# A graph-transformer kernel: tail work placed by a table of openings instead of an even pace

## The chip, the cores and the metric

The program runs on one core of one Trainium2 chip. The metric is device time in microseconds (us) of one execution. The engines are TensorE (PE: matmuls; its weight loads are PEld), VectorE (DVE), ScalarE (ACT), GpSimd (POOL) and SyncE (SP, which here only issues DMAs). [...]

## The reference, cut to what matters

Input x has 16 graphs of 1024 nodes and 128 features, adj is a sparse 1024 x 1024 adjacency matrix (about 8 neighbours a node). Four layers follow one another. Layers 0, 2 and 3 are attention over the neighbours with 8 heads of 16, each with a feed-forward part; layer 1 is graph attention (GAT) with one head. An attention layer is

```python
Q, K, V = h @ Wq, h @ Wk, h @ Wv                 # 8 heads of 16
attn = softmax(where(adj == 0, -inf, Q K^T / 4)) # over neighbours alone
x = layer_norm(h + attn @ V @ Wo + bo)
x = layer_norm(x + relu(x @ W1 + b1) @ W2 + b2)  # W1 is 128x256
...
h = x @ W; e = leaky_relu(h @ a_src + (h @ a_dst).T)
x = layer_norm(softmax(where(adj == 0, -inf, e)) @ h + x)   # layer 1
```

## The kernel before

**Units.** A layer is cut into two groups of 8 graphs (g = 0, 1) and 8 tiles of 128 nodes (t = 0 to 7), so there are 4 x 2 x 8 = 64 units (l, g, t); 48 are attention and 16 are GAT. Keys and values of all nodes of a group stand in a table in HBM. For each tile, rows of neighbours are gathered from that table by POOL's indirect DMA, one neighbour of each of 128 nodes a gather (1 MB in an attention layer).

**Parts.** A unit's gathers are worked off in parts: pairs of gathers, and one single gather that stands fourth (the "mixed" part, index 3). An attention unit has five parts, but six at t = 0 and four at t = 7. The main loop runs over all parts i of all units. In an attention unit one turn issues, in this order:

- `products(i)` (L958, DVE): gathered keys times queries, into one of four `pr` buffers;
- `summed(i-2)` (L1025, PE): weighted values added up over neighbours; frees `pr` buffers. Parts 0 and 1 of a unit are summed together, in the turn of part 3;
- after a unit's last part, `divided` first issues PE's sums of the exponentials (L1025, `ps<-ex,marks`);
- first call of `others()`;
- `exponentials(i)` (L981 reduce on DVE, L985 exp on ACT), then, in a unit's part 1, the next unit's `queries` and the load after it are put on their lists;
- second call of `others()`;
- `weighted(i-1)` (L1009, DVE), then `gathered(i+3)` (L946, POOL: issues the gathers three parts ahead into the ring of four `e` buffers);
- in a unit's part 1: the previous unit is closed (`divided` goes on with a reciprocal, L1062, and two multiplications, L1065, on DVE, which make `o` for the two halves of the graphs and create two tails);
- third call of `others()`.

I call a call of `others()` an **opening**: it is where all work that isn't the gather-multiply-sum stream is slipped in. A five-part unit has 15 of them.

**Tails.** A tail is a Python generator, `attention_tail(l, g, t, h, o)`, one for each half h of the 8 graphs (a: h = 0, b: h = 1). Each `yield` ends a step. In the kernel before a tail has 13 steps: transpose o (PE) with its copy (ACT) and the bias on x (ACT); Wo (8 matmuls); squares for the norm (ACT); `rstd` and scaling (ACT); transpose to x1; W1 with ReLU, both halves of the hidden layer; W2 (12 matmuls); squares; rstd and scaling; transpose to the new x; keys and values of two graphs; of two more; the table's DMA. Half b yields once at the start, and so runs one step behind a. In the last layer the end is a transpose back and an indirect DMA to `out` by POOL (L691), once for both halves. Before a unit is closed, all earlier tails must have handed back a flag "free" (given at the transpose to the new x; in the last layer it is never given, and the tails are run to their end).

**The pace.** At each closing, `pace` is set so that 13 less `LATE` (1 in layer 0, 2 in layers 2 and 3) steps are spread evenly over the openings of the unit. When it is due, `advance(tails)` moves every tail on by one step.

**The front.** Each opening also does one step of the first generator that has work among `fronts` (the next unit's `queries`, 4 steps: Wq for one half and the copy of q; 4 matmuls L909 that spread q over partitions and 4 copies L912; the same for the other half), `loads`, and, while layer 0 works on group 0, `at_leisure`: the transposes and projections of group 1 of the input.

**Buffers.** Four PSUM banks `ps` are shared by everything short-lived. `yps` has two banks, `acc` one tile, `pr` four, `e` four, and `f1` (the hidden layer) one.

Of the kernel before, what the change touches and what calls it, by code (L numbers as in the profile page):

```python
# [137 lines left out]
def sparse_path(ctx: ExitStack, tc: tile.TileContext, a: dict, out: bass.AP, flag):  # L138
# [20 lines left out]
    for j in range(J):  # L159
        q = slice(32 * j, 32 * j + 32)  # L160
# [452 lines left out]
    def normed(y, dve=False):  # L613

        z = twos.tile([P, GH, D], F32, tag="o", name="z")
        total = smalls.tile([P, GH], F32, tag="total", name="total")
        if dve:
            nc.vector.tensor_copy(z, y)
            nc.vector.tensor_tensor(z, z, y, ALU.mult)
            nc.vector.tensor_reduce(total, z, mybir.AxisListType.X, ALU.add)  # L620
            nc.vector.tensor_scalar(total, total, 1.0 / D, EPS, ALU.mult, ALU.add)
        else:
            for i in range(GH):
                nc.scalar.activation(  # L624
                    z[:, i, :], y[:, i, :], AF.Square, scale=D**-0.5, bias=root,
                    accum_out=total[:, i : i + 1],
                )
        yield
        rstd = smalls.tile([P, GH], F32, tag="rstd", name="rstd")
        nc.scalar.activation(rstd, total, AF.Ln)  # L630
        nc.scalar.activation(rstd, rstd, AF.Exp, scale=-0.5)
        if dve:
            nc.vector.tensor_tensor(
                z, y,
                rstd.rearrange("p (g o) -> p g o", o=1).to_broadcast([P, GH, D]), ALU.mult,
            )
            return z
        for i in range(GH):
            nc.scalar.activation(z[:, i, :], y[:, i, :], AF.Copy, scale=rstd[:, i : i + 1])  # L639
        return z  # L640
# [62 lines left out]
    def attention_tail(l, g, t, h, o):  # L703
        layer = LAYERS[l][0]
        p = {n: w[layer, n] for n in ATTN if (layer, n) in w}
        xt = xs[l, g, t][:, h]
        last = (l, g, t) == units[-1]
        dve = last and h > 0
        for _ in range(0 if last else h):
            yield  # L710
        oT = twos.tile([P, GH, P], F32, tag="oT", name="oT")
        turned(o, oT, dve=dve)

        if dve:
            nc.vector.tensor_scalar(xt, xt, p["bo"], None, ALU.add)
        else:
            nc.scalar.activation(xt, xt, AF.Identity, bias=p["bo"])
        yield
        ps = ybanks.tile([P, GH, D], F32, tag="yps", name="yps")
        for i in range(GH):  # L720
            nc.tensor.matmul(ps[:, i, :], oT[:, i, :], p["Wo"], start=True, stop=False)  # L721
            nc.tensor.matmul(ps[:, i, :], xt[:, i, :], centre, start=False, stop=True)  # L722
        yield
        z = yield from normed(ps, dve)
        yield
        x1 = twos.tile([P, GH, P], F32, tag="oT", name="x1")
        turned(z, x1, p["ln1_g"], p["ln1_b"], dve)
        yield
        f1 = (queries_of_shared if dve else hidden)().rearrange("p (f c) -> p f c", f=F)
        for f in range(F):  # L730
            ps = bank([P, GH * P])
            nc.tensor.matmul(  # L732
                ps, p["W1"][:, f * P : (f + 1) * P], x1.rearrange("p g n -> p (g n)"),
                start=True, stop=True,
            )
            if dve:
                nc.vector.tensor_scalar(
                    f1[:, f, :], ps, p["b1"][:, f : f + 1], 0.0, ALU.add, ALU.max
                )
            else:  # L740
                nc.scalar.activation(f1[:, f, :], ps, AF.Relu, bias=p["b1"][:, f : f + 1])  # L741
        yield
        ps = ybanks.tile([P, GH, D], F32, tag="yps", name="yps")
        for i in range(GH):
            for f in range(F):
                nc.tensor.matmul(  # L746
                    ps[:, i, :], f1[:, f, i * P : (i + 1) * P], p["W2"][:, f, :],
                    start=(f == 0), stop=False,
                )
            nc.tensor.matmul(ps[:, i, :], x1[:, i, :], centre, start=False, stop=True)  # L750
        yield
# [58 lines left out]
    def at_once(g):  # L810
# [12 lines left out]
        for t in range(T):  # L823
# [9 lines left out]
            while both:  # L833
                advance(both)
                yield

    def exponents():
        return exps.tile([P, MOST * G * H], F32, tag="ex", name="ex")

# [40 lines left out]
    def queries(u):  # L880
# [15 lines left out]
        for h in range(HF):  # L896
            q = ones_.tile([P, GH * D], F32, tag="q", name="q")
            ps = bank([P, GH, D])
            for i in range(GH):
                nc.tensor.matmul(  # L900
                    ps[:, i, :], xs[l, g, t][:, h, i, :], w[LAYERS[l][0], "Wq"],
                    start=True, stop=True,
                )
            nc.scalar.copy(q, ps.rearrange("p g d -> p (g d)"))  # L904
            yield
            pss = []
            for j in range(J):
                ps = bank([P, GH * D])
                nc.tensor.matmul(ps, rep_of(j), q[32 * j : 32 * j + 32], start=True, stop=True)  # L909
                pss.append(ps)  # L910
            for j in range(J):
                nc.scalar.copy(qs[u][:, j, h * GH * D : (h + 1) * GH * D], pss[j])  # L912
            yield

    def shared(u):

# [136 lines left out]
    def divided(u):  # L1053
# [9 lines left out]
        for h in range(HF):  # L1063
# [7 lines left out]
                ALU.mult,  # L1071
            )
            tails.append((attention_tail if heads > 1 else graph_tail)(l, g, t, h, o))
        nc.scalar.copy(both[:, 0, :], den)
        yield
        n = G * heads
# [2 lines left out]
    tails = []  # L1079
# [12 lines left out]
                free.append(gen)  # L1092

    pace = [0.0, 0.0]

    def idle():
        return slow if held[0] or not busy[0] else []

    def others():
        pace[0] += pace[1]  # L1100
        while pace[0] >= 1.0:
            advance(tails)
            pace[0] -= 1.0
        while True:
# [10 lines left out]
        for _ in range(eager[0]):  # L1115
            advance(idle())

    eager = [1]

    with tc.manual_schedule():  # L1120
# [39 lines left out]
        for i in range(len(parts) + 2):  # L1160
# [45 lines left out]
                    pass  # L1206
            if closing is not None and here:
                while any(gen not in free for gen in tails):
                    advance(tails)
                next(closing)  # L1210
                sizes, closing = closing, None
                passes = 3 if is_attention(u) else 4
                steps = STEPS if is_attention(done) else GRAPH_STEPS
                steps -= LATE[units[done][0]]
                pace[:] = 0.0, steps / (passes * sum(part[0] == u for part in parts) - 1)
            others()
            if i + 1 >= len(parts) or parts[i + 1][0] != u:

                while fronts:
                    advance(fronts)  # L1220
        while tails:
            advance(tails)
        for _ in closing:
# [438 lines left out]
```

## Time and profile before

| | us |
|---|---|
| median of 3 runs | 2250.97 (2247.27 to 2253.18) |
| the profiled execution | 2254.23 |
| its span in the profile | 2251.9 |
| busy: PE / DVE / ACT / POOL | 2043.1 / 1872.9 / 1528.3 / 1016.3 |
| PE weight loads | 1271.3 |
| mean granted clock of PE | 0.962 of full speed |

The span starts with the first instruction of the profile and ends with the last; 2.3 us of the execution's time lie outside it. Busy shares are averages over layers with different limits. [...] Layers show in the trace by the reciprocal (L1062) that closes each unit: layer 0's group 1 lies around 484 to 704 us, GAT from about 731 to 1042 us, layer 2 to about 1633 us, layer 3 to 2215 us, and then the last unit's tail to the end.

### The profile page before, as it was taken

To read this page: it belongs to the slowest core of one execution; us is meant where nothing else is said; L and a number is where in the kernel's file an instruction comes from. 1 tells how busy PE (TensorE), PEld (TensorE's weight loads), DVE (VectorE), ACT (ScalarE), POOL (GpSimd) and SP (SyncE) were. 2 spreads that over 40 slices of the span, in tenths; PEclk is the share of its full clock that TensorE was granted. 3 is DMA by queue.
4 is the path that set the end of the run, shared out by engine and by line. 5 is a ranking of instruction groups with operands and counts; after the bars stand their busy time and mean duration, and the time that the engine had idled before them with its cause. 6 is when DMAs were issued, how large, how long until landed. Compare 5 with 4: busy or idle time off the path is not lost.

```text
span 2251.9 us, 36507 instructions
## 1 busy us (share of the span) xinstructions
PE 2043.1 (91%) x13140; PEld 1271.3 (56%) x13140; DVE 1872.9 (83%) x1472; ACT 1528.3 (68%) x5041; POOL 1016.3 (45%) x699
## 2 busy tenths in 40 slices
PE   6589999899999999998999989999999998998986
PEld 5456665555555555554556655656655555555554
DVE  7897899888887577768988889989798998888893
ACT  3346777777777655555677777777777777676765
POOL 3343445354435368884343434334444544453540
PEclk8799999999999999999999999999999998999999
DMA  7897877778788699997997978887888788687860
GB/s 254 290 323 275 298 272 279 268 263 289 284 296 272 221 341 356 360 358 291 327 329 268 318 260 302 303 313 276 284 282 305 265 286 279 225 279 271 288 227 21
DMA packets 164700, 636.05 MB, mean 282 GB/s; under 512 B 34568, under 2 KB 37384, under 8 KB 116014
## 3 DMA queue, kind: packets, MB, share of 16 engines
q0 software_dynamic: 88720, 485.08, 61.0%
q1 hardware_dynamic: 75792, 148.57, 19.1%
q8 instruction: 105, 1.72, 0.3%
q14 instruction: 83, 0.68, 0.1%
HBM read 581.08 MB, written 92.34 MB: 299 GB/s over the span
## 4 chain that ended last, share of the span: by engine, by line
PE 41%; ACT 18%; issue 16%; DVE 11%; DMA 9%; POOL 5%; POOLq 0%; DVEq 0%; ACTq 0%
PE acc L1025 9%; DMA e<-table,idx 8%; PE yps L746 5%; PE ps L576 4%; POOL e L946 4%; PE ps L646 4%; ACT qr L912 4%; PE ps L732 3%; PE ps L909 3%; DVE pr L958 3%; ACT z L624 3%; DVE sc L981 3%; DVE pr L1009 2%; PE yps L750 2%; ACT z L639 2%
## 5 line engine op out<-in xcount | busy, mean ns | idle before, releaser
L946 POOL DMA_INDIRECT e<-table,idx x576 | 854.1, 1483 | 1101.8 <-DVE pr L1009 902.1
L1009 DVE TENSOR_TENSOR pr<-e,ex 128x2048 f32<-128x2048 f32 (+1 forms) x320 | 661.6, 2076 | 46.7 <-ACT ex L985 24.9
L958 DVE TENSOR_TENSOR pr<-e,qr 128x2048 f32<-128x2048 f32 x192 | 441.6, 2300 | 132.7 <-PE acc L1025 55.7
L1025 PE MATMUL acc<-pr,marks 128*32 128x512 f32 x2624 | 519.1, 608 | 14.8 <-DVE pr L1009 10.8
L981 DVE TENSOR_REDUCE sc<-pr 128x128 f32<-128x2048 f32 (+1 forms) x240 | 497.5, 2073 | 8.0
L624 ACT ACTIVATE z<-yps,root 128x128 f32<-128x128 f32 x888 | 317.5, 388 | 35.7 <-PE yps L765 17.2
L1025 PEld LDWEIGHTS acc<-pr,marks 128*32 128x32 f32 x2624 | 107.7, 110 | 269.4 <-issue 226.7
L639 ACT ACTIVATE z<-yps,rstd 128x128 f32<-128x128 f32 x888 | 254.0, 369 | 7.2
L746 PE MATMUL yps<-W,f 128*128 128x128 f32 x1520 | 251.8, 283 | 7.3 <-ACT f L741 1.8
L741 ACT ACTIVATE f<-ps,b 128x512 f32<-128x512 f32 x190 | 129.8, 695 | 157.6 <-PE ps L732 157.2
L746 PEld LDWEIGHTS yps<-W,f 128*128 128x128 f32 x1520 | 205.0, 192 | 51.0 <-issue 25.6
L576 PE MATMUL ps<-Wkv,xT 128*128 128x256 f32 x768 | 215.0, 419 | 20.0 <-ACT xT L652 16.7
L912 ACT COPY qr<-ps 128x512 f32<-128x512 f32 x384 | 197.3, 600 | 40.6 <-PE ps L909 40.5
L909 PE MATMUL ps<-q,rep 32*128 32x512 f32 x768 | 175.3, 661 | 34.7 <-ACT q L904 33.5
L732 PE MATMUL ps<-x,W 128*128 128x512 f32 x384 | 190.4, 620 | 12.5 <-ACT x L654 12.5
L624 ACT ACTIVATION_READ_ACCUMULATOR z<-yps,root 128x1 f32 x888 | 201.7, 227 | 0.0
L646 PE MATMUL ps<-ident,z 128*128 128x128 f32 x896 | 177.5, 299 | 25.5 <-ACT z L639 20.7
L646 PEld LDWEIGHTS ps<-ident,z 128*128 128x128 f32 x896 | 115.2, 142 | 149.2 <-ACT z L639 72.1
L580 ACT COPY kv<-ps 128x512 f32<-128x512 f32 x176 | 103.2, 589 | 131.9 <-PE ps L576 119.4
L576 PEld LDWEIGHTS ps<-Wkv,xT 128*128 128x128 f32 x768 | 146.5, 205 | 76.4 <-ACT xT L652 21.1
L721 PE MATMUL yps<-Wo,oT 128*128 128x128 f32 x768 | 160.3, 292 | 8.6 <-ACT oT L652 8.5
L722 PE MATMUL yps<-centre,x 128*128 128x128 f32 x768 | 155.5, 285 | 3.6
(176 smaller groups left out, 2597.7 us busy)
## 6 DMA issues: line engine op xcount, KB each, us to landing
table<-kv SPq DMA_DIRECT2D x88, 512.0 KB, 6.5
kept<-xT SPq DMA_DIRECT2D x96, 256.0 KB, 5.4
x<-kept SPq DMA_DIRECT2D x48, 512.0 KB, 9.2
qx<-qr SPq DMA_DIRECT2D x48, 256.0 KB, 6.7
e<-table,idx POOLq DMA_INDIRECT x576, 8.1
table<-kv SPq DMA_DIRECT2D x32, 256.0 KB, 7.7
qx<-qr SPq DMA_DIRECT2D x18, 384.0 KB, 9.1
qx<-qr SPq DMA_DIRECT2D x42, 128.0 KB, 8.1
```

What stands on the lines that cost most here:

```text
L576: nc.tensor.matmul(ps[:, k, :], x[:, i + k, :], w[LAYERS[l][0], "Wkv"], start=True, stop=True,)
L624: nc.scalar.activation(z[:, i, :], y[:, i, :], AF.Square, scale=D**-0.5, bias=root, accum_out=total[:, i : i + 1],)
L639: nc.scalar.activation(z[:, i, :], y[:, i, :], AF.Copy, scale=rstd[:, i : i + 1])
L646: nc.tensor.transpose(ps[:, i, :], z[:, i, :], ident)
L732: nc.tensor.matmul(ps, p["W1"][:, f * P : (f + 1) * P], x1.rearrange("p g n -> p (g n)"), start=True, stop=True,)
L746: nc.tensor.matmul(ps[:, i, :], f1[:, f, i * P : (i + 1) * P], p["W2"][:, f, :], start=(f == 0), stop=False,)
L912: nc.scalar.copy(qs[u][:, j, h * GH * D : (h + 1) * GH * D], pss[j])
L946: nc.gpsimd.indirect_dma_start(out=es[i][:, k, :], out_offset=None, in_=tables[l, g][:, :], in_offset=bass.IndirectOffsetOnAxis(ap=idx[:, ...
L958: nc.vector.tensor_tensor(prs[i][0][:, :n, :], es[i][:, :n, :ROW], qx[u].rearrange("p (o c) -> p o c", o=1) if (MIX, 0) in piece else of_p ...
L981: nc.vector.tensor_reduce(sc[:, :n, :], prs[i][0][:, :n, :].rearrange("p k (a d) -> p k a d", d=HD), mybir.AxisListType.X, ALU.add,)
L1009: nc.vector.tensor_tensor(prs[i][k0 // 2][:, :m, :].rearrange("p k (a d) -> p k a d", d=d), es[i][:, k0 : k0 + m, base : base + ROW].rearr ...
L1025: nc.tensor.matmul(outs[32 * j : 32 * j + 32], marks[:, mark, :], rhss, start=(chunk == mine[0]), stop=(chunk == mine[-1]),)
```

## The change

Three things are done.

1. Steps are made finer. A tail has 18 steps in place of 13: the bias on x is a step of its own, `rstd` is apart from the scaling (in both norms), and W1 and W2 are cut in two. Half b no longer yields at its start. The copies of the spread queries are cut in two, so `queries` has 6 steps in place of 4. GAT's tail gets one step more, through the shared `normed`.
2. After an attention unit is closed, the pace is no longer used. A table `PLAN` of 15 strings says for each opening which steps it does and in what order: "a" and "b" advance the oldest tail of that half by one step, "q" does one step of the front. The table holds 18 a, 18 b and 15 q. Past its end an opening does "abq". After GAT units the pace is used as before.
3. If a unit is closed before its predecessor's tails are free, the following strings are run, without leaving any out, in place of `advance(tails)`.

```diff
@@ normed
         nc.scalar.activation(rstd, rstd, AF.Exp, scale=-0.5)
+        yield
@@ attention_tail
-        for _ in range(0 if last else h):
-            yield
         oT = twos.tile([P, GH, P], F32, tag="oT", name="oT")
         turned(o, oT, dve=dve)
-
+        yield
...
                 nc.scalar.activation(f1[:, f, :], ps, AF.Relu, bias=p["b1"][:, f : f + 1])
-        yield
+            yield
...
             nc.tensor.matmul(ps[:, i, :], x1[:, i, :], centre, start=False, stop=True)
-        yield
+            if i % 2:
+                yield
@@ sparse_path
+    PLAN = (
+        "qaaqqbaba", "", "aq", "abb", "a", "qaba", "abbqabba", "", "baqbaba", "qqb", "bqaa", "", "b", "qbqqqbq", "ba",
+    )
@@ queries
                 nc.scalar.copy(qs[u][:, j, h * GH * D : (h + 1) * GH * D], pss[j])
-            yield
+                if j % 2:
+                    yield
@@ divided
             tails.append((attention_tail if heads > 1 else graph_tail)(l, g, t, h, o))
+            half_of[tails[-1]] = h
@@ others
+    def planned(beyond="abq"):
+        n = opening[0]
+        opening[0] += 1
+        for c in PLAN[n] if n < len(PLAN) else beyond:
+            if c == "q":
+                aside()
+                continue
+            for gen in tails:
+                if half_of[gen] == "ab".index(c):
+                    step(gen, tails)
+                    break
     def others():
+        if opening[0] is not None:
+            planned()
+            for _ in range(eager[0]):
+                advance(idle())
+            return
         pace[0] += pace[1]
         while pace[0] >= 1.0:
             advance(tails)
             pace[0] -= 1.0
+        aside()
...
@@ main loop, where a unit is closed
                 while any(gen not in free for gen in tails):
-                    advance(tails)
+                    if opening[0] is None:
+                        advance(tails)
+                    else:
+                        planned("ab")
...
+                if is_attention(done) and opening[0] is None:
+                    for gen in list(tails):
+                        if gen in free:
+                            for _ in gen:
+                                pass
+                            tails.remove(gen)
+                opening[0] = 0 if is_attention(done) else None
...
+        while opening[0] < len(PLAN):
+            planned()
         while tails:
             advance(tails)
```

Opening 0 is the third call in a unit's part 1, right after the closing. Openings 1 to 9 are those of parts 2, 3 and 4 of a five-part unit. Openings 10 to 14 lie in the next unit: three in its part 0, two in its part 1. No matrix product, copy or transfer is added or taken away. `aside` is the loop of the front, which stood in `others` before.

More of the change, by code (lines that the diff above doesn't have):

```diff
@@ L1094, in sparse_path, with step @@
     pace = [0.0, 0.0]
+    opening = [None]
+    half_of = {}
+    def step(gen, gens):
+        got = next(gen, "end")
+        if got == "end":
+            gens.remove(gen)
+        elif got == "free":
+            free.append(gen)
+    def planned(beyond="abq"):
[9 more added lines that the diff above has]
+                    break
     def idle():
@@ L1103, in others, with aside @@
             pace[0] -= 1.0
+        aside()
+        for _ in range(eager[0]):
+            advance(idle())
+    def aside():
         while True:
@@ L1114, in others @@
             break
-        for _ in range(eager[0]):
-            advance(idle())
     eager = [1]
```

## The prediction

> **What bounds the kernel now.** I read the page's busy times, then the waits of DVE by layer, then one unit's timeline on DVE, PE and ACT.
>
> ```profile
> PE 2043.1 (91%) x13140; PEld 1271.3 (56%) x13140; DVE 1872.9 (83%) x1472; ACT 1528.3 (68%) x5041; POOL 1016.3 (45%) x699
> ```
>
> PE looks like the limit. But in the timeline of one unit DVE runs its stream without a break except where something is late, so I take the unit's length from DVE and ask what breaks it. This is a five-part unit of layer 0, group 1 (DVE's timeline, from one closing to the next; idle time and releaser in brackets):
>
> ```profile
> 557.62 0.56 DVE L1062 RECIPROCAL both<-ps 128x64 f32<-128x64 f32 x1 [2.26 <-PE ps L1025]
> 558.21 1.29 DVE L1065 TENSOR_TENSOR o<-acc,both 128x512 f32<-128x512 f32 x2
> 559.42 2.28 DVE L958 TENSOR_TENSOR pr<-e,qr 128x2048 f32<-128x2048 f32 x1
> ...
> 572.78 2.29 DVE L958 TENSOR_TENSOR pr<-e,qr 128x2048 f32<-128x2048 f32 x1 [1.94 <-PE acc L1025]
> ...
> 594.02 0.56 DVE L1062 RECIPROCAL both<-ps 128x64 f32<-128x64 f32 x1 [2.06 <-PE ps L1025]
> ```
>
> The unit takes 594.02 - 557.62 = 36.40 us; 1.94 are lost where part 4's products wait for a `pr` buffer (PE's sum of parts 0 and 1 is late) and 2.06 where the closing waits for PE's sum of exponentials. DVE's own work is 36.40 - 4.00 = 32.40. In layer 3 another wait stands in the same unit (DVE's and POOL's timelines):
>
> ```profile
> 1820.44 0.55 DVE L1062 RECIPROCAL both<-ps 128x64 f32<-128x64 f32 x1
> ...
> 1842.57 2.29 DVE L958 TENSOR_TENSOR pr<-e,qr 128x2048 f32<-128x2048 f32 x1 [2.89 <-DMA e<-table,idx]
> ```
>
> ```profile
> 1823.38 2.10 POOL L691 DMA_INDIRECT out<-outs,places  x1 [0.30 <-ACT qr L912]
> 1829.38 1.75 POOL L946 DMA_INDIRECT e<-table,idx  x1 [3.89 <-DVE pr L1009]
> 1831.43 0.99 POOL L946 DMA_INDIRECT e<-table,idx  x1 [0.30 <-issue]
> ```
>
> The gather for the next unit's part 0 may go only when DVE has done `weighted` of part 1 (8.7 us after the closing), and its landing, 22.1 us after the closing, starts a remaining 13.5 us of DVE work. That is a floor of about 35.6 us which no order of the tails can lower, and the PE waits before it (parts 3 and 4) are hidden by it. The waits of layers 2 and 3 (DVE's waits, windows 1117 to 1633 and 1674 to 2203 us) say how much is left:
>
> ```profile
> DVE pr L958 <- PE acc L1025: 21.7, 12, 4.0
> DVE pr L958 <- DMA e<-table,idx: 17.4, 7, 5.5
> ```
>
> ```profile
> DVE pr L958 <- DMA e<-table,idx: 29.3, 10, 4.7
> DVE pr L958 <- PE acc L1025: 11.9, 7, 3.4
> ```
>
> One more thing speaks in layer 3 (stages; the last columns are clock, DMA share, GB/s):
>
> ```profile
> 1778.50:1785.30 6.80, 5.24 (x48) 3.24 (x44) 6.66 (x5) 5.14 (x17) 2.87 (x2) 1.00 0.43 145
> 1785.30:1792.10 6.80, 6.80 (x29) 5.25 (x27) 6.76 (x5) 4.36 (x9) 3.71 (x3) 0.50 0.80 275
> ```
>
> After 6.8 us in which PE was busy 77%, its clock is halved for 6.8 us, just when the next unit's tail begins.
>
> [...]
>
> **The change part by part.** Nothing is added or removed; all cost is in the order. I walk one five-part unit of layer 0, group 1 by the durations of the timeline: transpose of 4 blocks 0.55, Wq 1.06, spread of q 1.2 to 1.9, Wo 2.1, W1 0.93 a half, W2 1.5 a half, sum of parts 0 and 1 1.9, one part 0.95, exponentials' sum 1.1; ACT: copies 0.55 to 0.6, bias 0.72, squares 1.4, rstd 0.45, scaling 1.15, x1 and xn 0.78, ReLU 0.7, exp 0.3. Time zero is the closing. The same walk for the order before puts the end of the sum of parts 0 and 1 at 15.1 us; measured: 572.67 - 557.62 = 15.05. So I trust it to some tenths over such a stretch.
>
> *Openings 0 to 3.* PE: transpose a (2.5), spread of q (4.6), transpose b (5.1, after the first copy has freed a bank), Wo a (7.3), Wq (8.4), Wo b (10.5), then the sum: ends 12.4 where it was 15.05. The second spread, 1.9 us, has gone behind it to opening 5, which is most of this. Part 4's products start at 13.2, so the 1.94 us wait goes. ACT (copy, bias, four copies, copy, bias, squares, exp, rstd, copy, scaling, squares) is through at 12.6; no exp is late.
>
> *Openings 4 to 6, the fullest.* x1 a 13.8; two spread copies 15.15; ReLU a 16.5 and 17.65; PE stands 1.0 us before W2; scaling b 18.8; x1 b 20.6; the last two spread copies 21.7; ReLU b 23.9 (the single `f1` is free at 21.3); squares a 25.3. Only then comes the exp of part 4, issued after empty opening 7: 25.6. DVE wants it at 23.3 for `weighted` of part 4. A new wait of 2.3 us. Behind the waiting `weighted` stand the next part's products and gathers.
>
> *Openings 8 to 14.* ACT: rstd a, scaling a, squares b (28.6), new x a 29.3, a load's copy, rstd b, scaling b 31.45, two keys' copies 32.45, exp 32.75: DVE wants it at 32.3, 0.5 us more. PE's sum of exponentials ends at 34.1, the closing is at 35.05, so the 2.06 us wait goes too. Sum: 32.4 + 2.3 + 0.5 = 35.2 against 36.4: 1.2 us a unit; six such units: **-7 us**.
>
> *Layer 0, group 0.* The order of PE's queue shows where the 16 steps of `at_leisure` fall: between closings they stood 8, 6, 2 before and 8, 4, 1, 1, 1, 1 after. Each costs PE some 2.4 us. Units 1 and 2 lose 3 of them (7 us); units 3 to 5, where DVE also builds the slot lists, take them beside other work, and give back perhaps 3: **-4 us**.
>
> *Layer 2.* The PE waits (21.7 in the row above, and 5.5 at the closings) go, but the gathers' floor takes most of it; I take 0.5 us for each of 12 five-part units: -6 (bounds 0 and -20). Against it stand units that begin at half clock, see layer 3: three at 1.9: **0 us** together.
>
> *Layer 3.* The floor holds before and after, so nothing is gained, and two costs are new. POOL: `out` (2.10 us) stood behind the gather for part 4 and now stands before it (it is issued in opening 14), and it waits for the copy of opening 13. In my walk that copy is ready at about the moment when the gather could go, so the gather is 0 to 2.1 us late; part 4's wait is partly hidden by the 2.89 us of the floor. I take 0.3 us for 12 units: 4 (bounds 0 and 25). PE's clock: PE's work still thins out before the closing (from 27 us on about 5 us of it in 9), so the clock will be halved at least as often as before, when it hit about half of layer 3's closings (stages with a clock of 0.50 near 1785, 1857, 1895, 1912, 2034, 2072, 2116 and 2188 us). Before, a halved opening cost nothing: the unit that was closed at 1784.59 us, in the halved stretch above, is 1820.44 - 1784.59 = 35.85 us long. Now openings 0 to 6 are one chain: 6.8 us at half clock set PE back by 3.4 us, the sum of parts 0 and 1 ends at 15.8, still hidden by the floor, but the exp of part 4 comes at about 28.6 instead of 25.6, and DVE wants it at 26.7. 1.9 us for 8 of 14 units: 15 (bounds 0 and 27). **+19 us**.
>
> *GAT, the four-part units and the last tail*: GAT waits for gathers (its stage has DMA share 0.91); finer steps of the last tail interleave the same work on PE. I put 0 here, bounds -6 and +6.
>
> Sum: -7 - 4 + 0 + 19 = +8, on 2254.23 of the profiled execution (span 2251.9 and 2.3 outside), which lies 3.3 above the median of the runs. A change of the order shifts both alike; 2251 + 8 is 2259, and as the terms of layer 0 rest on no lost tenth at all I round up to **2260 us**.
>
> **Rivals.** *The exps are in time in layers 2 and 3 (faster).* The clock is halved no oftener than before and mostly for one window of 3.4 us, which sets PE back by 1.7 us and leaves the exp of part 4 within 0.6 us of its time: then layer 3 costs 4 and layer 2 gains 6: -7 - 4 - 6 + 4 = -13, **2238**. For it: many of layer 2's halvings can only be that short, since its stages show a mean clock of 0.93 and more. Against: the 6.8 us shown above.
>
> *Nothing shows.* The gathers' floor holds in layer 0 too once PE is quick, and what is won at the sums is lost at the exps: **2251**. For it: layer 0's unit is 36.4 and layer 3's 35.6, already close. Against: layer 0 shows almost no wait for gathers.
>
> *ACT's bunching decides everywhere (much slower).* Place: the exp of part 4 behind opening 6. Each us by which ACT is later than in my walk is paid once in each of 11 five-part units of layer 0 and in 24 of layers 2 and 3; the walk's margin there, 1.1 us, is used up. At 1 us: 11 + 24 on top of 2251: **2286**. It decides from about 0.5 us on. For it: some ten handoffs between PE and ACT lie in openings 5 and 6. Against: my walk hit 15.05.
>
> *The table is much better*: the exps are in time in layer 0 too: -13 - 11 x 2.3 = -38, **2213**. Against it is the chain of ReLUs and copies above.
>
> **How the numbers follow.** Slower in all 0.50: the forecast's own case (2254 to 2270) 0.32 and bunching 0.22, of which together some 0.04 fall under the bound; nothing 0.11; faster in layers 2 and 3 0.28; much better 0.07. Of a kernel like this about 0.3% (6.7 us) can be told from no change. That makes 0.35 faster, 0.15 same, 0.50 slower. Range 2224 to 2292: it leaves out most of the last case and about a tenth above. The forecast's own range is 2254 to 2270.
>
> **What would show it.** Right: in layer 0's units no wait of part 4's products for `acc` and none of the reciprocal for PE, instead a wait of about 2 us of `weighted` for the exp; in layer 3 waits of `weighted` for the exp in units that begin at half clock, and gathers for part 4 that go later. Wrong: five-part units of layer 0 over 36.4 us; no waits for the exp at all; DVE's waits for gathers in layer 3 much shorter or longer than 29 us.

## The result and the profile after

| | us |
|---|---|
| before, median of 5 runs on the same chip | 2250.97 (2244.65 to 2258.56) |
| after, median of 5 runs | 2223.84 (2220.67 to 2224.11) |
| ratio, 95% interval | 0.9883 [0.9854, 0.9913] |

The change is 1.2% faster. The forecast was 2260, on the wrong side, and the time lies just under the range's lower end of 2224. DVE's busy time hardly moves, 1872.9 to 1874.3 us, and PE's falls from 2043.1 to 2009.0 over the same 13140 matmuls (the first line of the page after; the clock is 0.958, before 0.962):

```profile
PE 2009.0 (90%) x13140; PEld 1265.3 (57%) x13140; DVE 1874.3 (84%) x1472; ACT 1520.1 (68%) x5041; POOL 1029.4 (46%) x699
```

So the gain is in what breaks DVE's stream. I cut both spans at the closings (DVE's reciprocals, counted from 0; the unit that closes a stage belongs to it, so the stage 0 to 8 holds the six-part unit that opens group 1). All stages are of the one profiled execution of each kernel. The last two columns belong to the experiments e9 and e12 below.

| stage (closings) | before | after | after - before | before, loads on POOL | after, loads on POOL |
|---|---|---|---|---|---|
| start to 0 | 161.8 | 164.6 | +2.8 | 164.3 | 166.0 |
| layer 0, group 0 (0 to 8) | 322.5 | 333.6 | +11.1 | 323.2 | 337.2 |
| layer 0, group 1 (8 to 15) | 247.1 | 228.6 | -18.5 | 252.2 | 228.5 |
| end of layer 0, GAT, first unit of layer 2 (15 to 32) | 351.2 | 356.5 | +5.3 | 355.2 | 359.7 |
| layer 2 (32 to 47) | 550.1 | 521.8 | -28.3 | 525.6 | 521.2 |
| layer 3 (47 to 63) | 582.6 | 575.3 | -7.3 | 541.5 | 548.4 |
| last tail | 36.6 | 41.8 | +5.2 | 38.2 | 41.7 |

**Layer 0, group 1.** The unit that answers to the one shown before (DVE's timeline of after; idle time and releaser in brackets; L1067 is the reciprocal, L963 the products, L1014 `weighted`):

```profile
566.17 0.55 DVE L1067 RECIPROCAL both<-ps 128x64 f32<-128x64 f32 x1
...
579.31 2.54 DVE L963 TENSOR_TENSOR pr<-e,qr 128x2048 f32<-128x2048 f32 x1
...
585.72 2.29 DVE L963 TENSOR_TENSOR pr<-e,qr 128x2048 f32<-128x2048 f32 x1 [0.42 <-ACT qr L916]
...
590.25 2.28 DVE L1014 TENSOR_TENSOR pr<-e,ex 128x2048 f32<-128x2048 f32 x1
...
597.41 2.29 DVE L1014 TENSOR_TENSOR pr<-e,ex 128x2048 f32<-128x2048 f32 x1 [0.36 <-ACT ex L990]
599.62 0.55 DVE L1067 RECIPROCAL both<-ps 128x64 f32<-128x64 f32 x1
```

The unit takes 33.45 us against 36.40. Both PE waits are gone (part 4's products at 579.31, the reciprocal at 599.62), 4.00 us, and only 0.42 + 0.36 came in their place. `weighted` of part 4, at 590.25, doesn't wait.

**Layers 2 and 3.** DVE's waits (total us, times, longest), layer 2 in the window 1118 to 1620:

```profile
DVE pr L963 <- ACT qr L916: 14.3, 2, 7.2
DVE pr L963 <- DMA e<-table,idx: 10.2, 8, 2.1
DVE pr L1014 <- ACT ex L990: 7.5, 6, 4.9
```

and layer 3, 1650 to 2180:

```profile
DVE pr L963 <- ACT qr L916: 21.0, 7, 6.0
DVE pr L963 <- DMA e<-table,idx: 16.3, 12, 2.6
DVE pr L1014 <- ACT ex L990: 6.6, 3, 5.3
DVE pr L963 <- PE acc L1030: 2.2, 4, 0.8
```

The waits for `acc` have nearly gone (21.7 and 11.9 before), those for gathers have fallen from 17.4 to 10.2 and from 29.3 to 16.3, and a wait is new that the prediction doesn't have: products wait for the copies of the spread queries, which the table has made late. The five-part units of layer 2 are 34.3 us long on average (36.8 before), those of layer 3 35.5 (36.3). The clock moved too: layer 2 of before has seven stretches at half clock (five of 3.4 us and two of 6.8, 31 us together, mean clock 0.97 in its window), and after has none (1.00).

**What moved the gathers.** In a unit of layer 2 of the kernel before (closings at 1194.18 and 1230.56) POOL issued the two gathers for the next part 0:

```profile
1203.12 1.73 POOL L946 DMA_INDIRECT e<-table,idx  x1 [6.30 <-DVE pr L1009]
1205.15 0.99 POOL L946 DMA_INDIRECT e<-table,idx  x1 [0.30 <-ACT qr L912]
```

and SP's queue sent this (same unit):

```profile
1204.39 1.54 SPq L922 DMA_DIRECT2D qx<-qr  x2
1206.46 0.60 SPq L875 DMA_DIRECT2D x<-kept  x1
1225.66 4.62 SPq L568 DMA_DIRECT2D kept<-xT  x2
```

That is 384 KB of shared queries and 512 KB of x for later units, in the flight of that gather. They stand in part 1 of the next unit in the program (about 1224), but SP has nothing else to do, runs ahead, and sends them from 1204.39 on, while ACT makes the last copies of the queries (1203.79 to 1205.83). The products of the next part 0 then start late on DVE:

```profile
1217.11 2.29 DVE L958 TENSOR_TENSOR pr<-e,qr 128x2048 f32<-128x2048 f32 x1 [3.05 <-PE yps L750]
```

The view names a product of PE (L750), but these products of DVE read nothing of it. PE's last sum before them ended at 1211.11, ACT's last query copy at 1205.83, so the gather is what is left. From 1207 to 1217 us SP's queue moved 1.00 MB and the gathers' queue 2.34 MB, 335 GB/s together.

In a unit of after (closings at 1188.09 and 1221.13) the same loads leave just before the closing:

```profile
1216.04 3.87 SPq L568 DMA_DIRECT2D kept<-xT  x2
1220.08 2.07 SPq L927 DMA_DIRECT2D qx<-qr  x2
1222.19 0.76 SPq L879 DMA_DIRECT2D x<-kept  x1
```

Here the `kept` writes hold the loads: the table puts these writes ahead of the loads in SP's queue, the last query copy ended at 1207.81, and the loads follow right behind the writes. The gathers of this unit went at 1196.95 and 1198.98, and part 0's products started at 1207.35 without a wait. From 1200 to 1207.3 us SP's queue moved nothing and the gathers' queue 2.50 MB, 342 GB/s: about the same rate in all, now the gathers' alone. The unit is 33.04 us long, against 36.38. In both kernels the two gathers of nearly every five-part unit of layer 2 go 8.9 and 11 us after the closing; where part 0's products wait for them, they begin mostly 22.4 to 22.7 us after it before (20.9 to 25.2 in all), and 20.2 to 21.3 after.

Layer 3 has no `kept` writes. There SP of after still sends the first piece of the queries in the gather's flight, 13 to 16 us after the closing in most units; the rest leaves about when the gather lands (unit with closings at 1758.66 and 1794.51, SP and DVE):

```profile
1774.88 6.71 SPq L927 DMA_DIRECT2D qx<-qr  x2
1781.64 0.58 SPq L879 DMA_DIRECT2D x<-kept  x1
```

```profile
1781.06 2.29 DVE L963 TENSOR_TENSOR pr<-e,qr 128x2048 f32<-128x2048 f32 x1 [2.68 <-ACT qr L916]
```

So layer 3 keeps most of its wait at this place, for the gather in one unit and for the query copies in another.

**Layer 0, group 0.** Three units (closings 2 to 5) are about 42.8 us long against 38 to 39. The last of them, DVE of after, is

```profile
341.34 0.56 DVE L1067 RECIPROCAL both<-ps 128x64 f32<-128x64 f32 x1
...
355.38 2.29 DVE L963 TENSOR_TENSOR pr<-e,qr 128x2048 f32<-128x2048 f32 x1 [0.81 <-PE acc L1030]
...
363.81 2.29 DVE L963 TENSOR_TENSOR pr<-e,qr 128x2048 f32<-128x2048 f32 x1 [2.68 <-ACT qr L916]
...
376.18 0.77 DVE L427 COPY little<-ps 32x24 f32<-32x24 f32 x4 [3.36 <-PE ps L413]
...
384.29 0.56 DVE L1067 RECIPROCAL both<-ps 128x64 f32<-128x64 f32 x1
```

and its stages (columns as in the prediction; the third from the end is the clock):

```profile
334.70:341.50 6.80, 4.50 (x47) 3.04 (x40) 6.58 (x16) 2.31 (x9) 0.00 (x0) 1.00 0.96 355
```

```profile
344.30:351.10 6.80, 6.80 (x29) 5.30 (x26) 6.74 (x4) 4.13 (x10) 0.89 (x1) 0.50 0.57 223
```

The table leaves PE little around the closing (4.50 us busy in 6.80, and 1.53 of the 3.40 from 340.9 on, where it waits 2.88 us for ACT's copy of q), and the next unit's opening runs at half clock (0.50 in the second row); that happened near 214, 259, 300, 344 and 385 us, for 6.8 us each time. The sum for `acc`, the query copies and the slot lists' sums are all late in turn.

### The profile page after: what moved, and what is told of

Same layout as the page of the kernel before. It is cut to its first block, busy times and chain, and to the rows that moved or that the text cites. A ratio compares the mean times of both kernels' runs of the same rounds, so it can differ in the third digit from the quotient of the medians.

```text
span 2222.3 us, 36516 instructions
## 1 busy us (share of the span) xinstructions
PE 2009.0 (90%) x13140; PEld 1265.3 (57%) x13140; DVE 1874.3 (84%) x1472; ACT 1520.1 (68%) x5041; POOL 1029.4 (46%) x699
## 4 chain that ended last, share of the span: by engine, by line
PE 57%; DVE 14%; ACT 12%; issue 9%; DMA 5%; POOL 3%; POOLq 0%; DVEq 0%; ACTq 0%
PE acc L1030 14%; PE ps L647 6%; PE ps L913 6%; PE yps L745 6%; PE ps L576 5%; PE ps L731 5%; DMA e<-table,idx 4%; DVE pr L1014 4%; PE yps L721 3%; PE yps L720 3%; DVE pr L963 3%; PE yps L749 3%; DVE sc L986 2%; ACT f L740 2%; POOL e L951 2%
## 5 line engine op out<-in xcount | busy, mean ns | idle before, releaser
L951 POOL DMA_INDIRECT e<-table,idx x576 | 882.2, 1532 | 1017.7 <-DVE pr L1014 750.9
L1014 DVE TENSOR_TENSOR pr<-e,ex 128x2048 f32<-128x2048 f32 (+1 forms) x320 | 661.5, 2076 | 59.5 <-ACT ex L990 31.9
L963 DVE TENSOR_TENSOR pr<-e,qr 128x2048 f32<-128x2048 f32 x192 | 443.4, 2309 | 116.4 <-ACT qr L916 71.3
L1030 PE MATMUL acc<-pr,marks 128*32 128x512 f32 x2624 | 506.5, 608 | 30.7 <-DVE o L1070 19.1
L916 ACT COPY qr<-ps 128x512 f32<-128x512 f32 x384 | 202.4, 595 | 30.4 <-PE ps L913 24.2
L580 ACT COPY kv<-ps 128x512 f32<-128x512 f32 x176 | 103.3, 593 | 173.2 <-PE ps L576 162.6
L576 PE MATMUL ps<-Wkv,xT 128*128 128x256 f32 x768 | 205.2, 409 | 15.2 <-ACT xT L653 13.1
L913 PE MATMUL ps<-q,rep 32*128 32x512 f32 x768 | 186.4, 688 | 13.4 <-ACT q L908 11.9
L624 ACT ACTIVATION_READ_ACCUMULATOR z<-yps,root 128x1 f32 x888 | 191.7, 216 | 0.0
L647 PE MATMUL ps<-ident,z 128*128 128x128 f32 x896 | 152.4, 286 | 14.0 <-ACT z L640 10.9
L647 PEld LDWEIGHTS ps<-ident,z 128*128 128x128 f32 x896 | 106.1, 141 | 77.0 <-ACT z L640 49.6
```

The costliest lines, as they stand in the source:

```text
L576: nc.tensor.matmul(ps[:, k, :], x[:, i + k, :], w[LAYERS[l][0], "Wkv"], start=True, stop=True,)
L624: nc.scalar.activation(z[:, i, :], y[:, i, :], AF.Square, scale=D**-0.5, bias=root, accum_out=total[:, i : i + 1],)
L647: nc.tensor.transpose(ps[:, i, :], z[:, i, :], ident)
L951: nc.gpsimd.indirect_dma_start(out=es[i][:, k, :], out_offset=None, in_=tables[l, g][:, :], in_offset=bass.IndirectOffsetOnAxis(ap=idx[:, ...
L963: nc.vector.tensor_tensor(prs[i][0][:, :n, :], es[i][:, :n, :ROW], qx[u].rearrange("p (o c) -> p o c", o=1) if (MIX, 0) in piece else of_p ...
L1014: nc.vector.tensor_tensor(prs[i][k0 // 2][:, :m, :].rearrange("p k (a d) -> p k a d", d=d), es[i][:, k0 : k0 + m, base : base + ROW].rearr ...
```

## The experiments

The ratios are against the kernel before on the same chip. The theory at the start was: quick PE sums and late queries pay by themselves (T). Rival D: the gain of layers 2 and 3 is a side effect of SP's transfers, out of the way of the gathers.

**e1: the table writes moved.** `table<-kv` of layer 2 is held back to openings 2 and 3.

```diff
-            nc.sync.dma_start(table..., kv...)
+            held_back.append((h, write))      # issued by SP at openings 2 (a) and 3 (b)
```

> The changed kernel, but the table writes of layer 2 (two of 512 KB a unit) are issued in openings 2 and 3 of the next unit, about where the kernel before had them, in place of opening 14; everything else keeps its place. Theory D (the gain of layer 2 comes from moving these writes away from the gather for the next unit's part 0): layer 2's five-part units go back from 34.3 to about 36.5 us, waits of products for gathers rise from 10 to over 20 us in layer 2, and the whole is about 25 us slower than the changed kernel (ratio to before 0.998 or more). Theory Q (the gain comes from the order on PE and ACT alone): layer 2 keeps its 34.3 us units, ratio about 0.988.

Measured: 2247.52, 0.9975 [0.9958, 0.9991]. It doesn't test what it was made for, as SP's timeline of this run shows:

```profile
1184.49 0.97 SPq L884 DMA_DIRECT2D x<-kept  x1
1185.50 1.50 SPq L586 DMA_DIRECT2D table<-kv  x2
```

SP sent the writes right behind the load as in after, in spite of their later place. Five-part units of layer 2 stayed at 34.3 us but for one of 45.3; the loss is in that one and one in layer 3. In the first, ACT waited for the buffer of a write (`ACT kv L580 <- DMA table<-kv`, 13.2 us at one place). **e6** did it again with ACT's queue, whose timeline shows the writes at 1198.28 and 1199.96, about where SP sent them in before. The gathers for the next part 0 went at 1200.65 and 1202.68, so the writes run just ahead of them and into the start of their flight.

> The changed kernel with layer 2's two table writes (1 MB a unit) issued by ACT's queue at openings 2 and 3, so that they really go in the time of the gather for the next unit's part 0 (from SP's queue they had gone as before, since SP runs ahead of the other engines). Theory D: layer 2's five-part units rise from 34.3 to over 35.5 us and the waits for gathers in layer 2 from 10 to over 20 us; the whole is 12 to 25 us slower than the changed kernel. Theory Q: within 6 us of the changed kernel.

Measured: 2231.52, 0.9879 [0.9835, 0.9923]; layer 2's five-part units stay at 34.4 us on average. The table writes, at the moment that they had in before, aren't what hurts the gather. Writes sent as late in its flight as the loads were not tried.

**e2: queries early again.** Of the table, three strings:

```diff
-"abb" (3), "qaba" (5), "abbqabba" (6)
+"qabbq" (3), "aba" (5), "abbabba" (6)
```

> The changed kernel with the second half of the queries moved from openings 5 and 6 to opening 3, so that no copy of a spread query stands in openings 5 and 6. Theory Q1 (queries late pay, because PE's sum of parts 0 and 1 is no longer behind the second spread): that sum ends about 1.9 us later, waits of part 4's products for acc come back (over 15 us in layers 2 and 3 together), the waits of products for the copies of the queries (71 us in the whole trace) go; the net is 0 to 20 us slower than the changed kernel. Theory Q2 (the lateness of the queries only costs): those 71 us go and nothing comes back, 20 to 40 us faster than the changed kernel, ratio 0.975.

Measured: 2307.24, 1.023 [1.018, 1.0279]. DVE's waits in layer 2 (1140 to 1660):

```profile
DVE pr L1014 <- ACT ex L990: 29.1, 25, 5.7
DVE pr L963 <- PE acc L1030: 17.6, 9, 3.4
```

That is slower than either expectation allowed. The waits for the query copies went (14.3 to 5.5 us in layer 2) and those for `acc` came back, but most of the loss is at the exps, which the copies push back in 25 places: this is the bunching of ACT that the prediction feared, in a table that differs by two letters' places.

**e4: the coarse steps by the same table.** The new yields are joined to the step before them, so that letters keep their places.

```diff
-        yield
+        yield "more"      # run on; the tail passes the next letter
```

> The changed kernel with the tail's finer steps joined again: at the first letter of a group that was one step before (transpose and bias; rstd and scaling; both halves of W1; both halves of W2) the whole group is issued, and the letters of its other pieces do nothing. The table and the queries stay. If the fineness brings the gain (ACT's and PE's pieces interleaved), the ratio goes back to 0.995 or more. If the table's places do, it stays within 0.985 to 0.991.

Measured: 2269.01, 1.0055 [1.0038, 1.0073]; 0.5 to 2.2 us more than after in the five-part units of layer 0's group 1 and of layer 2, no more on average in layer 3. Fine steps are worth about 1.7% here (1.0055 against 0.9883). They cut no instruction: they let other work stand between a tail's instructions.

**e7: the kernel before with late queries**, 13 coarse steps and the pace kept; three idle turns before the second half of the queries, from layer 0's group 1 on.

> The kernel before, its pace and its coarse steps kept, with one edit: the second half of the next unit's queries comes three openings later (from group 1 of layer 0 on), as the table has it. If the lateness of the queries makes most of the gain (PE's sum of parts 0 and 1 is earlier, and qx goes later on SP), the ratio is 0.992 or less, and part 4's waits for acc (37 us in layers 2 and 3) fall under 12 us. If the table as a whole is needed, the ratio is 0.997 or more.

Measured: 2366.03, 1.0469 [1.044, 1.0498]. DVE's waits in layer 2 (1150 to 1700):

```profile
DVE pr L1011 <- ACT ex L987: 28.6, 12, 3.3
DVE both L1064 <- PE ps L646: 22.1, 7, 3.2
DVE pr L960 <- ACT qr L912: 19.8, 12, 7.3
```

Late queries alone are a loss in these coarse steps.

**e3, e11: layer 0's group 0.** e3 gives the leisure steps one unit more at full rate (`eager` for u < 3); e11 runs this group by an even pace with the fine steps, half b four steps behind.

> The changed kernel, in which each opening of unit 2 does an extra step of group 1's input too (as units 0 and 1 do), so that at_leisure is done by unit 2 or 3 instead of 5. If the 14 us that units 2 to 5 of layer 0 lost come from its late steps on ACT and PE, units 3 to 5 return from 42.8 to about 38.5 us and the whole gains 5 to 12 us against the changed kernel (ratio 0.983 to 0.986). If they come from the slot lists' waits and PE's halved clock at each of these closings, units 3 to 5 stay over 41 us and the ratio stays at 0.988.

> The changed kernel, but in layer 0's group 0 the tails go by an even pace again (18 fine steps, half b four steps behind a); the table begins with layer 0's group 1. If the +11 us of group 0 come from the table's lean openings before the closing (half clock of PE at each next closing) and from its late queries: units 2 to 5 return from 42.8 to about 39 us, the stretches of clock 0.50 at each closing vanish, 8 to 12 us less than after, about 2213. If they come from the place of the 16 leisure steps and of the slot lists' sums instead, which stay as in after or nearly so: units stay at 42 us or more, 2220 to 2230.

Measured: 2231.36, 0.9894 [0.9846, 0.9942] and 2264.37, 1.0039 [1.0024, 1.0055]. In e3 the unit before the three lost 5.5 us and the three won 2.1 to 2.7 each: the stage 0 to 8 is 0.4 us shorter than after's, and the mean clock stays at after's 0.92 from 250 to 340 and from 340 to 430 us (before, 0.98 and 0.96). In e11 the units are 43 to 46 us long. Neither brings back 39 us, so the cause of the +11 us is not settled: half clock, late copies and slot lists' sums come together, and no run parts them.

**e8: the query step first in opening 6.**

> The changed kernel with the last two copies of the queries moved to the front of opening 6 (q before a and b). The waits of products for the query copies (71 us in the trace) should fall by more than half; the chain to the exp of part 4 gets 1.1 us longer. If the waits for the copies are on the path, 5 to 20 us faster than the changed kernel; if the exp takes over, no change or up to 10 us slower.

Measured: 2239.09, 0.9911 [0.9877, 0.9944]: no gain.

**e5, e9: the two loads taken out of SP's queue**, in the kernel before, with nothing of the change. e5 has them issued by ACT, e9 by POOL:

```diff
-                nc.sync.dma_start(qx[u][at], qs[u][at, j, :])
+                nc.gpsimd.dma_start(qx[u][at], qs[u][at, j, :])
...
-        nc.sync.dma_start(xs[units[u]]..., kept[l, g][t]...)
+        nc.gpsimd.dma_start(xs[units[u]]..., kept[l, g][t]...)
```

> The kernel before, with two kinds of transfer issued by ACT's queue in place of SP's: the mixed part's queries (qx, 384 KB) and the load of x (512 KB). ACT issues them in its order, at a unit's part 1, whereas SP, with nothing to hold it back, issues them some 10 us after the closing, while the gather for the next unit's part 0 is under way. Theory D (in the changed kernel late queries and SP's order keep these transfers out of that gather's time, and this is where layers 2 and 3 gain): waits of products for gathers in layers 2 and 3 fall from 47 us to under 25, and the time falls by 10 to 20 us. Theory Q (the order on PE and ACT is all): no change within 0.3%, or a little slower for ACT's issuing.

> The kernel before, with the transfers qx<-qr and x<-kept issued by POOL, in the program's place between the gathers, instead of by SP. Nothing of the change. Theory D (SP, which runs ahead, puts these two transfers into the flight of the gather for the next part 0, and that is what makes it land late in layers 2 and 3): they now go with the gather of part 2, which has more time; DVE's waits for gathers fall from 17.4 (layer 2) and 29.3 us (layer 3) to under 8 and under 15, five-part units of layer 3 fall from 36.3 to about 35 us, ACT is not held up as in the version that issued from ACT, so the kernel is 10 to 20 us faster than before (2230 to 2242). Rival F (the gather lands late because of its own 1 MB and the moment when DVE frees its buffer): waits for gathers stay at 15 and 25 us or more, time within 7 us of before. Rival G (POOL is held up by waiting for the copies of the queries or for buffers of x): gathers are issued later, slower than before.

Measured: e5 2272.87, 1.0059 [1.0044, 1.0075]; e9 **2200.04, 0.975 [0.9721, 0.9779]**. In e5 no wait for a gather is left in layer 2, and most of layer 3's five-part units fall to about 34 us, but in layer 2 DVE's waits for `acc` rise from 21.7 to 55.7 us: ACT's own work comes late where it issues. PE's waits in its layer 2 (1117 to 1640; the same wait was 17.9 us before in this window):

```profile
PE ps L909 <- ACT q L904: 31.6, 13, 4.0
```

POOL has little other work to hold up: before, it was busy 45% of the span, and 854.1 of its 1016.3 us were the gathers themselves. A unit of layer 3 of e9, on POOL:

```profile
1855.64 2.80 POOL L946 DMA_INDIRECT e<-table,idx  x1 [3.93 <-DVE pr L1009]
1858.43 1.14 POOL L922 DMA_DIRECT2D qx<-qr  x2
1859.51 0.61 POOL L875 DMA_DIRECT2D x<-kept  x1
```

and on DVE:

```profile
1828.30 0.55 DVE L1062 RECIPROCAL both<-ps 128x64 f32<-128x64 f32 x1
...
1848.55 2.29 DVE L958 TENSOR_TENSOR pr<-e,qr 128x2048 f32<-128x2048 f32 x1 [0.97 <-issue]
...
1862.00 0.55 DVE L1062 RECIPROCAL both<-ps 128x64 f32<-128x64 f32 x1
```

The loads now stand where the program has them, behind a gather that has time. The unit falls to 33.70 us here, and to 32.6 in most of the stage: DVE's own 32.4, with the old steps and the old pace. Waits for gathers in layer 2 fall from 17.4 to 1.4 us; in layer 3 none is listed.

**e14, e15: the moment or the queue, and which load.** e14 keeps POOL's queue but puts the loads right behind the gather for the next part 0 in layers 2 and 3; e15 moves only `x<-kept`.

```diff
                 gathered(i - 1 + AHEAD)
+                if here and i == begun + 2 and early(u + 1):
+                    if u + 1 < len(units):
+                        shared(u + 1)
+                    advance(loads)
...
```

> The kernel before with the two loads on POOL's queue, but in layers 2 and 3 right behind the gather for the next part 0, so at about the moment at which SP sent them. If the moment counts (they share the gather's flight): DVE's waits for gathers come back to 15 us and more in each of layers 2 and 3, and the time to 2240 or more. If it is the queue that counts [...]: waits for gathers stay near those of e9, the wait may come at the gather for part 1 behind them instead, time within 10 us of e9's 2200.

> The kernel before with only x<-kept (512 KB) issued by POOL; qx<-qr (384 KB in two pieces) stays with SP. By bytes the larger load should bring somewhat more than half of e9's gain of 59 us: 2222 to 2232. If qx alone is what hurts (it goes first, into the middle of the flight): within 10 us of before.

Measured: e14 2247.29, 1.0 [0.9982, 1.0018]; e15 2241.48, 0.9967 [0.9952, 0.9981]. DVE's waits of e14, layer 3 (1670 to 2200):

```profile
DVE pr L958 <- DMA e<-table,idx: 25.7, 21, 2.5
DVE pr L958 <- PE acc L1025: 10.7, 8, 3.4
```

The whole gain of e9 is gone on the same queue (2247.29 against 2200.04): the moment decides, not the queue. But the wait stands elsewhere than before. Here are part 0's and part 1's products of one unit:

```profile
1867.89 2.29 DVE L958 TENSOR_TENSOR pr<-e,qr 128x2048 f32<-128x2048 f32 x1 [2.26 <-DMA e<-table,idx]
...
1876.18 2.29 DVE L958 TENSOR_TENSOR pr<-e,qr 128x2048 f32<-128x2048 f32 x1 [1.48 <-DMA e<-table,idx]
```

Of the 25.7 us, ten waits (11.1 us) are for the gathers of part 0, which POOL issued ahead of the loads, and eleven (14.6 us) for those of part 1 behind them; before, nearly all of the 29.3 us were for part 0. So with two queues, in before, gathers and SP's loads together moved about what the gathers move alone in after (335 and 342 GB/s), and part 0's products waited for their gathers; with one queue, in e14, more than half of the wait stands at the gathers behind the loads. How the DMA queues share the rate is not shown beyond that. One reserve: at this place POOL also waits for the query copies (2.27 us in one unit), so part of the wait for part 1 is a later issue and not a longer flight; no run parts the two. Moving x alone (e15) brings less than was expected (waits for gathers 21.7 and 27.4 us in layers 2 and 3); qx alone wasn't tried.

**e10, e12, e13: what can be added.** e10 is the change with leftover tails run to their end at the closing; e12 is the change with the loads on POOL; e13 has both.

```diff
-                if is_attention(done) and opening[0] is None:
+                if is_attention(done):
```

> The changed kernel; at each closing of an attention unit what is left of tails that have handed back 'free' is run to its end at once, as the branch does that now serves only GAT's successors. It matters in units where the table isn't through at the closing (after units of four parts, where the six-part unit follows). Theory (six-part units of 45 us are long because two sets of tails overlap in them, and the new tail's a-steps find the old tail first): six-part units fall by 1 to 3 us each, 5 of them, so 5 to 12 us less than after, about 2215. Rival (six-part units are long because the lead of 15 openings ends and ACT is behind with the query copies; the rest of the tails is small): within 3 us of after, 2221 to 2227.

> The changed kernel, with the transfers qx<-qr and x<-kept issued by POOL in the program's place. If the change's gain in layers 2 and 3 was only that it moved these loads (theory D): it has little more to gain in layer 2 (34.2 us a five-part unit stays), but layer 3, where SP still sends qx between 13 and 23 us after the closing, falls from 35.4 to about 33 us: some 2200 us, no better than the kernel before with the same edit (2200). If table and loads add up: layer 0's group 1 keeps its gain of 22 us over before and layer 3 falls by 25 to 30: about 2190. Rival: POOL is held up by waiting for the late copies of the queries, and gathers for part 4 go later: 2215 or more.

> The changed kernel with both: leftover tails run to their end at the closing, and the two loads issued by POOL. If the two edits are independent: 9 us less than after_loads_pool (e10 was 9.5 us below after), about 2185.

Measured: e10 2214.32, 0.9814 [0.9784, 0.9843]; e12 2205.02, 0.9806 [0.978, 0.9832]; e13 **2183.68, 0.9714 [0.9687, 0.9741]**, the fastest of all. In e10 two of the six-part units, in layer 2's group 1 and layer 3's group 0, fall from 45.1 to 41.8 us. With the loads on POOL the table as it stands is no gain (e12 0.9806, e9 0.975). Were table and loads independent, e12 would be at 0.9883 x 0.975 = 0.964; it is at 0.9806, so some 38 us are counted twice. The stage table shows where: with the loads on POOL the table changes layers 2 and 3 by -4.4 and +6.9 us, with the loads on SP by -28.3 and -7.3. In layer 0's group 1 it gives -23.7 against -18.5: there its gain is its own. What the table does in layer 3 once the gathers are out of the way (e12, 1640 to 2160):

```profile
DVE pr L1014 <- ACT ex L990: 13.4, 5, 5.8
DVE pr L963 <- ACT qr L916: 8.1, 3, 6.0
DVE pr L963 <- DMA e<-table,idx: 4.0, 5, 1.1
```

It has traded waits for PE against waits for ACT (e9's list for layer 3 has 8.3 us for `acc` and 6.7 for exps).

## Why the prediction was wrong, point by point

- **"A floor of about 35.6 us which no order of the tails can lower": this step failed, and in layer 2 alone it turns the sum.** I took the gather's landing for its own price. It was the price of a gather with 896 KB of other loads in its flight. Layer 2's five-part units of after, 34.3 us on average and down to 33.0, are already below the floor, with the gathers issued at the same moments and landing 1 to 2 us earlier in most units; units of 32.6 us in layer 3 of e9, with the steps untouched, lie below it too, and e14 brings the time back with the moment of the loads. The change does move these loads: in layer 2 behind the `kept` writes, which the table puts ahead of them in SP's queue. I followed POOL's queue past the moved steps, not SP's. It cost the forecast layer 2 (0 said, -28.3 measured). How much of the -28.3 is the gathers' and how much the sums' is open: the waits for `acc` went at the same time, 21.7 us by the list, and so did the half clock; a version of after with the loads back in the flight wasn't tried.
- **Half clock in layer 3 (+15): the second step that failed.** It came (clock 0.50), at about every second closing and mostly for 6.8 or 10.2 us. That thin work of PE brings it was my estimate from the one stretch shown. But the waits for exps sum to 6.6 us, not 15, and the wait that half clock brings is for the query copies, 1.7 to 2.7 us in each of six five-part units. It stands at the products that wait for the gather in the other units, so it takes that wait's place and isn't added: the six average 35.4 us, the other six 35.5. So layer 3 came out at -7.3 where +19 was said, with the floor nearly in place there. Three of the eight stages that the prediction lists (1912, 2034 and 2072) begin 19 to 30 us behind a closing, not at it, and the 77% before the one shown are 3.40 us of 3.40 and then 1.84 of 3.40. In layer 2, where it put three such openings, the clock was never halved.
- **The new wait of 2.3 us for the exp of part 4: mis-sized.** The sum of parts 0 and 1 ended 577.26 - 566.17 = 11.1 us after the closing (12.4 said). The exp of part 4 ran from 589.45 to 589.78, so it ended 23.6 after the closing (25.6 said), and DVE wanted it at 24.1. That ACT takes its instructions in the program's order was the walk's assumption, and here it did: copy of `o` at 568.33, four query copies from 569.65, the squares of a from 588.08, then this exp. The direction was right (both PE waits go); the walk was 2.0 us too long up to this exp, 1.3 of it already at the sum. It also left out that the next part 0's products need the late query copies: 0.42 us here. The -1.2 a unit became about -3.0. This is the rival "much better", at 0.07, whose mechanism came true in layer 0.
- **`out` before the gather for part 4 (4 us): about right.** Four waits of part 4's products for a gather, 2.9 us together, stand in units of layer 3 where `out` went first; in e12 the five waits listed, 4.0 us, are all at part 4.
- **Layer 0, group 0 (-4): +11.1, and 2.8 more before it.** That the leisure steps would be hidden was wrong, or too small beside half clock at five closings, which I had priced in layer 3 only; which of them it was stays open. Layer 0 as a whole (-7.4, -11 said) is near its forecast by luck: two misses of opposite sign.
- **GAT and the last tail (0, bounds -6 and +6):** +5.3 in the stage around GAT and +5.2 at the end; I didn't look for the cause of either. Not foreseen at all: six-part units of layers 2 and 3 grow by 3 to 5 us, where the table's openings end before the unit does and old tails meet new ones; e10 takes this back in two of the three.

## What to carry to other kernels

In this kernel a gather's landing time was that of its company: in layer 2, where part 0's products waited for it, they began mostly 22.4 to 22.7 us after the closing with 896 KB of loads in its flight, and 20.2 to 21.3 without. So before a late landing is called a floor, list what every other queue sends between its issue and its landing, and when the change will make those transfers ready. SP, with no other work, sent the loads at 1204.39 for a place at about 1224 before, beside the last query copies, and at 1220.08 in after, right behind the `kept` writes of 1216.04; so here the moved writes moved the loads behind them too. Loads that nobody needs soon did best here on a queue whose order holds them where there is slack (e9, 2200.04 us against 2259.08). And where two changes remove waits of the same units, try them together before adding up their gains.

## What was not expected of the hardware

- A later place in SP's program was no later in time: in e1 the writes went at 1185.50, right behind the load at 1184.49, as they do in after (1188.51 behind 1186.97).
- With 896 KB of loads in the flight of part 0's gathers DVE stood idle for 3.05 us in the unit shown and up to 5.5 in others; 59 us in the kernel (2259.08 on e9's chip to 2200.04) hang on the moment at which two kinds of load are sent.
- Issuing the same loads from ACT raised PE's waits for the copy of q in layer 2 from 17.9 to 31.6 us and DVE's for `acc` from 21.7 to 55.7 (e5).
- PE's clock was halved for 6.8 us after 3.40 us in which it was busy 1.53 us (after, from 340.9) or 1.84 us (before, from 1781.9).
